# A projection computed by seven products of quarters, and a group norm applied by ScalarE, in a two-layer attention kernel

## The chip, the cores and the metric

The kernel runs on one core of a Trainium2 chip. A core has several engines with a queue of instructions each: TensorE (PE in the profile) multiplies matrices into PSUM banks of 128 partitions by 512 floats; VectorE (DVE) and ScalarE (ACT) work element by element on SBUF and PSUM; [...]SyncE (SP) mostly issues transfers (DMA). An engine takes its queue in order. An instruction that waits for another engine, or for a transfer, therefore holds up everything behind it in its own queue.

The metric is the time on the device in microseconds (us), the median over runs.

## The reference

The input is a batch of eight images, `x` of 8 x 512 x 32 x 32 in float32: 512 channels and T = 1024 positions per image. Two layers follow each other, cut here to what matters:

```python
# layer 0
h = group_norm(xf, gn_w, gn_b)                        # 32 groups of 16 channels
qkv = jnp.einsum('oc,bct->bot', qkv_w, h) + qkv_b[None, :, None]
q, k, v = jnp.split(qkv.reshape(b * 8, -1, T), 3, axis=1)   # 8 heads of 64 channels
q, k, v = fake_quant(q), fake_quant(k), fake_quant(v)       # to 255 levels, one scale per tensor
w = softmax(jnp.einsum('bct,bcs->bts', q * scale, k * scale), axis=-1)
a = jnp.einsum('bts,bcs->bct', w, v).reshape(b, c, T)
a = jnp.einsum('oc,bct->bot', proj_w, a) + proj_b[None, :, None]
x = xf + a
# layer 1, one head over all 512 channels
t = group_norm(x, gn_w, gn_b).reshape(B, C, T).transpose(0, 2, 1)
q, k, v = t @ wq.T + bq, t @ wk.T + bk, t @ wv.T + bv
attn = softmax(q @ k.transpose(0, 2, 1) / sqrt(C), axis=-1)
out = x + ((attn @ v) @ wp.T + bp).transpose(0, 2, 1)
```

## The kernel before

Until about 600 us a first phase computes q, k and v of all images and stores them to DRAM. The second phase, which the change touches, runs two streams of work side by side.

The first stream is the attention of layer 0, the generator `attention()`. Its units are (image b, pair of heads j, half hf of the queries, block s of 128 keys). A unit is a score matmul `st`, its exponential `pt` on ACT, a split of `pt` into a high and a low half of 16 bits (`two`, the low half by DVE; the high half by ACT or POOL), and the products `av` (with v) and `sm` (row sums). After all keys of a pair, `finish` copies the result to the `ao` tile, and `divide` (a DVE instruction, due about 20 us later) divides it by the row sums.

The second stream, `others()` (line 1900), takes image after image through the projection of layer 0 (`project`, line 1296), the group norm of layer 1 (`norm1`, line 1344) and the rest of layer 1 (`layer1`, line 1655). Layer 1 uses folded weights: `g` = (WqT Wk) h, scores `s` between g and h, values `v2ps` with Wp Wv, and `o`, the sum over the values. Each `yield` of this stream lets the attention go on by one step, so layer 1 of image b runs while the heads of image b+1 are attended to. The projection and norm of image b+1 run inside the last `o_run` of image b (`between`, line 1761): the projection's two halves after the fifth product of `o_run`'s seven, the two small steps of the norm after the sixth and seventh, the rest at the beginning of `layer1(b+1)`, whose first matmuls are `g` again.

**Seven products.** The blocks `g`, `v2ps`, `s` and `o` multiply two matrices by quarters. Each matrix is cut into 2 x 2 quarters, and seven products of sums of quarters give the result, where the plain form takes eight (Winograd's form of Strassen's method). The sums of the right-hand matrix (`t1 = h12 - h11`, `t2 = h22 - t1`, `h22 - h12`, `t4 = h21 - t2`) are formed by DVE; those of weights are formed once. The helper `seven` (line 1393) alternates between two PSUM banks, adds some products up in the bank, and lets a product wait (`awaits`) until the bank has been read. The work is tiled by 128 x 256: a product is 8 matmuls.

The projection of before is in plain form: for each half of the positions and each of four blocks of 128 output channels, four matmuls of 128 x 512 (`pj`) add up in a bank; DVE adds the bias and x, `evict`, into the `h` tile (`xts[b]`); a transfer stores it for layer 1's residual; and `bn_stats` takes the statistics for the norm. `norm1` gets the group means and variances through two tiny matmuls, and then DVE applies the norm in eight instructions of 128 x 512, four for each half, `(h - mean) * rstd`. The first half's four are issued at once, the second half's four are put off.

**Order.** A planner, the class `InOrder` (line 72), fixes the order of each engine's queue when the program is built. `dve`, `act` and `pe` each keep a planned time `t`. `do(cost, work)` issues an instruction now. `later(name, cost, work, ready, within)` puts a chore on a list with a time from which it may begin and one at which it is due. `fill` issues those chores that fit before a given time, the earliest first, and `settle(name)` issues all chores of that name at once, in their order:

```python
def do(self, cost, work, ready=None):
    ready = pe.t + 0.25 if ready is None else ready
    self.fill(ready)
    self.t = max(self.t, ready) + cost
    work()
```

The planner's costs are only estimates; the chip runs what was issued in the order in which it was issued. TensorE's order is that of the calls of `mm` (line 209 in the profile). Instructions issued through the planner are put down to line 91.

**Buffers.** The `h` tile holds x, then x plus the projection, then the normed input of layer 1. The tile `sums` holds the projection's weights (`wp`, 1 MB), and after the projection the sums of quarters of the normed input. Both are loaded late in layer 1 of the image before (line 1755). Scores and projection share the PSUM banks `ps_s`, of which `pair_ps` hands out two banks at a time; `g`, `v2ps`, `s` and `o` have the banks of `ps_o`.

Of the kernel before, what the change touches and what calls it, by code (L numbers as in the profile page):

```python
# [9 lines left out]
F32 = mybir.dt.float32  # L10
# [8 lines left out]
P = 128  # L19
# [39 lines left out]
def attn_pair_kernel(  # L59
# [166 lines left out]


    def norm_steps(
        src, dst, wcol, bank, nm, ccs=range(CC), fine=False, put=None, mv=None, apply=None
    ):  # L230

        n, c0 = len(ccs), ccs[0]
        put = put or (lambda hf, cost, work: work())
        if mv is None:
            st, mv = stat_tiles(n, nm)
            for i, cc in enumerate(ccs):
                for hf in range(NH):
                    dve.bn_stats(st[:, i, hf, :], src(cc, hf))  # L240
                aggregate(mv, st, i)
                if fine and i + 1 < n:
                    yield
        yield
# [12 lines left out]
        dve.do(0.6, offsets)  # L257
        yield
        ps2 = bank(f"gps2_{nm}")[:, 0:n]
        mm(ps2, lhsT=gavg, rhs=d, start=True, stop=True)  # L260
        rstd = small.tile([P, n], F32, tag=f"grstd{n}", name=f"grstd_{nm}")
        dve.do(0.15, lambda: dve.tensor_scalar(rstd, ps2, EPS, None, ALU.add))
        nc.gpsimd.tensor_tensor(rstd, rstd, mhalf[:, 0:n], ALU.pow)
        dve.do(
            0.15, lambda: dve.tensor_mul(rstd, rstd, vec[:, wcol + c0 : wcol + c0 + n]), dve.t + 1.4
        )
        if apply is not None:
            off = small.tile([P, n], F32, tag=f"goff{n}", name=f"goff_{nm}")
            dve.scalar_tensor_tensor(off, mean, -1.0, rstd, ALU.mult, ALU.mult)
            for i, cc in enumerate(ccs):  # L270
                apply(cc, rstd[:, i : i + 1], off[:, i : i + 1])
                yield
            return
        for hf in range(NH):
            for i, cc in enumerate(ccs):
                put(hf, 0.5, lambda i=i, cc=cc, hf=hf: dve.tensor_scalar(
                    dst(cc, hf), src(cc, hf), mean[:, i : i + 1], rstd[:, i : i + 1],
                    ALU.subtract, ALU.mult,
                ))
                if fine and i % 2 == 1:  # L280
                    yield
        if not fine:
            yield
# [23 lines left out]
    with ExitStack() as fast:  # L307
# [710 lines left out]
        def attention():  # L1018
# [138 lines left out]
            def finish(b, j, hf, u):  # L1157

                nm = f"{b}_{j}"
                if hf == 0:  # L1160
                    if b:
                        settle("ao")
                    ao[b, j] = aop.tile([P, NH, 512], F32, tag="ao", name=f"ao_{nm}")
                    if b == 0 and j % 2 == 1:
                        rss[b, j] = kept_u[:, 0:2].rearrange("p h k n -> p h (k n)")
                    else:
                        rss[b, j] = l1p.tile([P, NH, 512], F32, tag="rs", name=f"rs_{nm}")
                aot, rs = ao[b, j], rss[b, j]
# [15 lines left out]

                def divide():
                    dve.scalar_tensor_tensor(aot, aot, scl[:, 2:3], rs, ALU.mult, ALU.mult)

                def spread():
                    r = rcs[:, n * 16 : (n + 1) * 16]
                    dve.tensor_add(r, apart[:, 0, :], apart[:, 1, :])  # L1190
                    dve.reciprocal(r, r)
                    nc.sync.dma_start(rs_d[n].rearrange("r (p k) -> (r p) k", k=16), r)
                    for i, r in enumerate(HALF):
                        nc.sync.dma_start(
                            rs[r], rs_d[n][2 * i : 2 * i + 2, :].partition_broadcast(CH)
                        )
# [67 lines left out]
                dma(xts[b][:, :, bass.ts(hf, 512)], x_v[b, :, :, bass.ts(hf, 512)])  # L1264

        def load_wp(b, dma):
            wps[b] = l2p.tile([P, CC, C], F32, tag="sums", name=f"wp0_{b}")
            dma(wps[b], w_sq[WP0])

        def load_first(u):  # L1270

# [21 lines left out]
            for t, src in zip(wm_tiles(b), wm_d):  # L1293
                act.dma_start(t, src)

        def project(b, bank=bank):

            settle("ao")  # L1300
            st, mvs[b] = stat_tiles(CC, f"b{b}")
            wp0 = wps.pop(b)
            for hf in range(NH):
# [40 lines left out]
        def norm1(b, bank=bank):  # L1344
# [3 lines left out]

            def put(hf, cost, work):
                if hf == 0:  # L1350
                    dve.do(cost, work)
                else:
                    dve.later("h", cost, work, within=27.0)

            def put_sum(hf, i, work):
                if hf == 0:
                    dve.later("t4" if i == 3 else "t", elements(512), work, within=10.0 + 2.0 * i)
                else:
                    put(hf, elements(512), work)

            for n, _ in enumerate(norm_steps(
                at, at, V_GN1W, bank, f"b{b}", put=put, mv=mvs[b]
            )):
                if n == 2:
                    sums[b] = l2p.tile(
                        [P, 3, NH, CC // 2, 256], F32, tag="sums", name=f"sums2_{b}"
                    )
# [22 lines left out]
            dve.later("o", 0.25, spread, pe.t + 4.0, 5.0)  # L1390
            return rs

        def seven(nm, pairs, keep, whole, add, bank=bank):

            nonlocal turn
            turn ^= 1  # L1400
            x, y = (bank(f"{nm}_{i}").rearrange("p (t n) -> p t n", t=2) for i in range(2))

            def product(n, ps, start):
                left, right = pairs[n]
                k = left.shape[1]
                for t in range(2):
                    for i in range(k):
                        mm(
                            ps[:, t, :], lhsT=left[:, i, bass.ts(t, P)], rhs=right[:, i, :],
                            start=start and t == 0 and i == 0, stop=(i == k - 1),  # L1410
                            skip_group_check=True,
                        )
# [4 lines left out]
                (5, x, False, whole, None),  # L1417
            )
            for i, (n, ps, start, out, m) in enumerate(work):
                awaits(free[(i + turn) % 2])  # L1420
                product(n, ps, start)
                free[(i + turn) % 2] = out(ps) if m is None else out(m, ps)
                yield i + 1

        free = [0.0, 0.0]
        turn = 0

        def slots(gq):
# [226 lines left out]
        def layer1(b, steps):  # L1655
# [46 lines left out]
            for hf in range(NH):  # L1702
# [52 lines left out]
                if last and b + 1 < B:  # L1755
                    load_wp(b + 1, act.dma_start)
                    load_x2(b + 1, act.dma_start)
                if done >= B:
                    load_x1(b, hf, 0, 1, rx, aop)
                settle("v")  # L1760
                between = [lambda: iter((1,)), lambda: iter(()), lambda: iter(())]
                if b + 1 < B and last:

                    def first():
                        nonlocal ahead
                        yield -1
                        yield from project(b + 1, score_bank)
                        yield 2
                        ahead = norm1(b + 1, score_bank)
                        next(ahead)  # L1770
# [534 lines left out]
```

## Time and profile before

| | |
|---|---|
| time, median of 3 runs | 2559.91 us (2559.35 to 2560.78) |
| time of the profiled execution | 2559.32 us |
| its span, first to last instruction | 2557.2 us |
| granted TensorE clock, mean | 0.999 of full speed |
| HBM traffic over the span | 94 GB/s |
| PE busy, 0 to 600 us | 586.2 us |
| PE busy, 600 to 2400 us | 1782.7 us |
| PE busy, 2400 to 2557 us | 147.0 us |

Engines overlap, so busy times don't add up to the span. In the profile's timelines a line is a group of equal instructions close to each other: its start in us from the start of the span, the time from the start of its first to the end of its last instruction, the engine, the line of the code, the operation, output and inputs by the program's names, their shapes, and how many there are. Square brackets at the end hold the engine's idle time just before and what ended it. So `[5.64 <-PE st L209]` is an idle time of 5.64 us that ended when TensorE's `st` was there. In the table of groups the numbers after the bar are the whole busy time, the mean of one instruction in ns, and the idle time before them.

The projection's matmuls `pj` are 512 records with 224.1 us. The norms on DVE, 64 instructions, take 35.4 us in all: 0.455 us at the least, 0.538 in the median, 1.259 at the most.

### The profile page before, as it was taken

What the parts mean: (1) busy time and instruction counts of PE and PEld (TensorE: products, weight loads), DVE (VectorE), ACT (ScalarE), POOL (GpSimd) and SP (SyncE); (2) the same over time, 40 slices, a digit from 0 to 9 for tenths busy, and PEclk for the clock granted to TensorE, in tenths of its full rate; (3) what the DMA queues carried; (4) which work ended last, traced back from release to release, by engine and by line L of the source; (5) the groups of instructions that cost most, each with busy time, mean ns of one, the idle gap of its engine ahead of it and who ended that gap; (6) DMA issues with size and microseconds to landing.
All of it is one profiled execution on the core that took longest, in us unless ns stands there. A gap on an engine that the chain in (4) does not pass through costs nothing.

```text
span 2557.2 us, 38727 instructions
## 1 busy us (share of the span) xinstructions
PE 2515.9 (98%) x15670; PEld 1746.2 (68%) x15670; DVE 1897.6 (74%) x2747; ACT 1346.5 (53%) x1685; POOL 186.0 (7%) x167
## 2 busy tenths in 40 slices
PE   8999999999999999999999999999999999999998
PEld 4788888873357756775777577667756775777787
DVE  7887776668887778777877787777778777885544
ACT  3332223319857655665666466656655665664121
POOL 0000000001100001000100100010101000100000
PEclk9999999999999999999999999999999999999999
DMA  4533333236622232223313222322232123212211
GB/s 168 177 142 125 131 124 122 109 131 162 162 88 63 79 116 85 58 74 122 98 57 100 92 79 78 110 92 63 79 112 88 55 71 128 96 42 80 87 38 39
DMA packets 160717, 250.70 MB, mean 98 GB/s; under 512 B 27152, under 2 KB 93712, under 8 KB 159120
## 3 DMA queue, kind: packets, MB, share of 16 engines
q1 hardware_dynamic: 125792, 182.81, 21.6%
q10 hardware_dynamic: 30560, 57.71, 6.5%
q0 software_dynamic: 4176, 7.60, 1.7%
q8 instruction: 125, 2.05, 0.3%
q14 instruction: 64, 0.52, 0.1%
HBM read 153.64 MB, written 86.28 MB: 94 GB/s over the span
## 4 chain that ended last, share of the span: by engine, by line
PE 85%; DVE 5%; ACT 2%; issue 1%; DMA 1%; POOL 0%; SPq 0%; ACTq 0%; DVEq 0%
PE s L209 15%; PE o L209 13%; PE qkps L209 12%; PE pj L209 8%; PE av L209 8%; PE v2ps L209 7%; PE vps L209 6%; PE g L209 6%; PE st L209 4%; PE sm L209 3%; DVE two L91 2%; ACT pt L91 1%; PE fold L209 1%; DVE h L91 1%; DVE acc L91 0%
## 5 line engine op out<-in xcount | busy, mean ns | idle before, releaser
L91 ACT ACTIVATE pt<-st,esc 128x1024 f32<-128x1024 f32 x467 | 496.4, 1114 | 332.1 <-PE st L209 317.6
L91 DVE TENSOR_TENSOR two<-pt,two 128x1024 f16<-128x1024 f32 x467 | 561.5, 1216 | 131.0 <-POOL two L1092 100.7
L91 ACT CAST two<-pt 128x1024 f16<-128x1024 f32 x346 | 350.8, 1055 | 6.9 <-ACT p L91 5.1
L1092 POOL CAST two<-pt 128x1024 f16<-128x1024 f32 x112 | 146.0, 1304 | 1409.4 <-PE sm L209 746.3
L209 PE MATMUL av<-two,v 128*32 128x512 f16 x3968 | 245.9, 381 | 2.5 <-DVE two L91 2.1
L209 PE MATMUL s<-g,h 128*128 128x256 f32 x1024 | 233.4, 380 | 0.0
L209 PE MATMUL pj<-ao,wp 128*128 128x512 f32 x512 | 224.1, 595 | 0.6 <-DVE h L91 0.6
L209 PEld LDWEIGHTS s<-g,h 128*128 128x128 f32 x1024 | 192.9, 190 | 31.0 <-issue 4.3
L91 ACT ACTIVATE u_ring<-qkps,qkbt 128x512 f32<-128x512 f32 x89 | 60.9, 685 | 243.8 <-PE qkps L209 219.3
L209 PEld LDWEIGHTS <-v 128*32 128x32 f16 x3968 | 91.8, 96 | 140.0 <-issue 66.7
L209 PEld LDWEIGHTS pj<-ao,wp 128*128 128x128 f32 x512 | 96.0, 190 | 122.5 <-issue 110.8
L209 PE MATMUL s<-g,sums 128*128 128x256 f32 x768 | 178.4, 381 | 0.2 <-DVE p L91 0.2
L209 PE MATMUL o<-p,v 128*128 128x256 f32 x768 | 175.2, 382 | 1.0 <-DVE p L91 1.0
L209 PE MATMUL st<-q,k 64*128 64x512 bf16 x1024 | 163.4, 382 | 11.9 <-ACT pt L91 7.5
L209 PEld LDWEIGHTS o<-p,v 128*128 128x128 f32 x768 | 144.3, 190 | 27.1 <-issue 5.7
L209 PEld LDWEIGHTS s<-g,sums 128*128 128x128 f32 x768 | 144.7, 190 | 24.2 <-issue 4.6
L209 PE MATMUL sm<-two,ones 128*32 128x512 f16 x1984 | 136.0, 379 | 0.0
L209 PEld LDWEIGHTS <-k 64*128 64x128 bf16 x1024 | 34.8, 94 | 143.8 <-issue 142.2
L209 PE MATMUL qkps<-half,w_high 128*128 128x512 f32 x480 | 132.4, 398 | 0.0
L209 PE MATMUL qkps<-half,w_mix 128*128 128x512 f32 x480 | 130.6, 394 | 1.0 <-DVE half L91 1.0
L209 PE MATMUL qkps<-half,w_low 128*128 128x512 f32 x480 | 130.5, 394 | 0.0
L209 PE MATMUL v2ps<-wm,h 128*128 128x256 f32 x512 | 119.9, 383 | 1.9 <-ACT g L91 1.3
(226 smaller groups left out, 3902.2 us busy)
## 6 DMA issues: line engine op xcount, KB each, us to landing
rs<-rs_d SPq DMA_DIRECT2D x76, 256.0 KB
x<-in_x_dram SPq DMA_DIRECT2D x32, 512.0 KB
q_d<-wa SPq DMA_DIRECT2D x32, 512.0 KB
k_d<-wa SPq DMA_DIRECT2D x32, 512.0 KB
v_d<-v_ring SPq DMA_DIRECT2D x32, 512.0 KB
raw<-q_d SPq DMA_DIRECT2D x32, 512.0 KB
raw<-k_d SPq DMA_DIRECT2D x32, 512.0 KB
x_d<-h SPq DMA_DIRECT2D x64, 256.0 KB
```

The costliest lines, as they stand in the source:

```text
L91: ins = self.latest = op(*args, **kw).ins
L209: ins = nc.tensor.matmul(ps, lhsT=lhsT, rhs=rhs, **kw).ins
L1092: copy(two[:, 0], pt)
```

## The change

Two things are changed.

**The projection of images 1 to 7 in seven products.** `project` of image 0 stays as it was, but also has DVE form the four sums of the quarters of its weights (`combine_wp`), which are stored to DRAM. From the next image on, `load_wp` brings three quarters of the weights and three of the stored sums in three transfers of 1.5 MB in all; the fourth sum, 256 KB, comes into the room of layer 1's values by a transfer at the beginning of `project_seven`. The sums of quarters of `ao` are formed by DVE: the first two instructions after the division of the second pair of heads (`first_sums`), two more at the beginning of the projection, and four of 128 x 256 in each half. The bias is added to x beforehand, by four ACT instructions of 128 x 1024 (`add_bias`). The seven products of a half use the two banks of one `pair_ps` tile (`alone`), and each of them is added by DVE to its quarter of `h`, seven additions where there were four. The statistics of a half, four instructions, follow the sixth and seventh product; the stores are 256 wide.

**Layer 1's norm on ACT.** For all images the eight norms are ACT instructions with a scale and an offset, `h * rstd + off`; DVE computes the offset, one small instruction. Those of the first half are issued at once, and those of the second half are put on ACT's list (due within 22 us in place of 27). The four sums of quarters of each half stay on DVE. The second half's sums first settle all norms of that half.

```diff
     def norm_steps(
...
+        if scaled:
+            off = small.tile([P, n], F32, tag=f"goff{n}", name=f"goff_{nm}")
+            dve.do(0.15, lambda: dve.scalar_tensor_tensor(
+                off, mean, -1.0, rstd, ALU.mult, ALU.mult
+            ))
         for hf in range(NH):
             for i, cc in enumerate(ccs):
-                put(hf, 0.5, lambda i=i, cc=cc, hf=hf: dve.tensor_scalar(
-                    dst(cc, hf), src(cc, hf), mean[:, i : i + 1], rstd[:, i : i + 1],
-                    ALU.subtract, ALU.mult,
-                ))
+                if scaled:
+                    put(hf, 0.6, lambda i=i, cc=cc, hf=hf: act.activation(
+                        dst(cc, hf), src(cc, hf), AF.Identity, bias=off[:, i : i + 1],
+                        scale=rstd[:, i : i + 1],
+                    ))
...
                 def divide():
                     dve.scalar_tensor_tensor(aot, aot, scl[:, 2:3], rs, ALU.mult, ALU.mult)
+                    if b and j == 1:
+                        first_sums(b)
...
         def load_wp(b, dma):
-            wps[b] = l2p.tile([P, CC, C], F32, tag="sums", name=f"wp0_{b}")
-            dma(wps[b], w_sq[WP0])
+            wps[b] = w = l2p.tile([P, 6, CC // 2, C // 2], F32, tag="sums", name=f"wp0_{b}")
+            dma(w[:, 0:2].rearrange("p i k n -> p (i k) n"), w_sq[WP0][:, :, 0 : C // 2])
+            dma(w[:, 2], w_sq[WP0][:, CC // 2 :, C // 2 :])
+            dma(w[:, 3:6], wp_d[:, 0:3])
...
+        def combine_wp():
...
+            for args in (
+                (s1, a21, a22, ALU.add), (s2, s1, a11, ALU.subtract),
+                (s3, a11, a21, ALU.subtract), (s4, a12, s2, ALU.subtract),
+            ):
+                dve.later("wc", elements(512), lambda args=args: tt(*args), within=20.0)
+            dve.later("wc", 0.0, lambda: nc.sync.dma_start(wp_d, wc[:, 0:4]), within=20.0)
+
+        def add_bias(b):
+            for cc in range(CC):
+                act.later("xb", 1.05, lambda cc=cc: act.activation(
+                    xts[b][:, cc, :], xts[b][:, cc, :], AF.Identity,
+                    bias=vec[:, V_PB0 + cc : V_PB0 + cc + 1],
+                ), pe.t + 17.0, 24.0)
+
+        def first_sums(b):
+            for cc in range(CC // 2):
+                h = ao[b, cc]
+                dve.later("at", elements(512), lambda h=h: tt(
+                    h[:, :, 256:512], h[:, :, 256:512], h[:, :, 0:256], ALU.subtract
+                ), within=30.0)
+
+        def project_seven(b, room):
+
+            settle("at")
             settle("ao")
+            act.settle("xb")
...
+            act.dma_start(s4, wp_d[:, 3])
...
+            for k in range(2):
+                dve.do(elements(512), lambda k=k: second(k))
+
+            for hf in range(NH):
...
+                at = pair_ps(f"pj_{b}_{hf}")
+                banks = iter((at[:, 0, :], at[:, 1, :]))
+
+                def into(q, row, col, full, hf=hf):
+
+                    def add(ps):
+                        there = dve.do(elements(512), lambda: tt(q, ps, q, ALU.add))
+                        if full is not None:
+                            nc.sync.dma_start(x1_d[b][row][hf][:, :, col * 256 : (col + 1) * 256], q)
+                        return there
+
+                    return add
+
+                def stats(oc, hf=hf):
+                    dve.bn_stats(st[:, oc, hf, :], xts[b][:, oc, bass.ts(hf, 512)])
+                    if hf == NH - 1:
+                        aggregate(mvs[b], st, oc)
...
+                for step in seven(
+                    f"pj_{b}_{hf}",
+                    ((a11, h11), (a12, h21), (s2, th), (s3, h11), (s1, t1), (s4, h22), (a22, h21)),
+                    lambda n, ps: keeps[n](ps), into(q12, 0, 1, 1), lambda n, ps: adds[n](ps),
+                    lambda _: next(banks), True,
+                ):
+                    if step in (1, 2):
+                        for k in range(2):
+                            h = (h11, h21)[step - 1][k]
+                            args = (h, th[k], h) if step == 1 else (h, h, th[k])
+                            dve.do(elements(256), lambda args=args: tt(*args, ALU.subtract))
+                    for oc in {6: (2, 3), 7: (0, 1)}.get(step, ()):
+                        dve.later("pj", 0.62 + 0.2 * hf, lambda oc=oc, stats=stats: stats(oc), within=4.0)
+                    chore()
+                if hf + 1 < NH:
+                    yield -1
+            settle("pj")
...
             def put(hf, cost, work):
                 if hf == 0:
-                    dve.do(cost, work)
+                    act.do(cost, work, dve.t + 0.1)
                 else:
-                    dve.later("h", cost, work, within=27.0)
+                    act.later("h", cost, work, within=22.0)
 
             def put_sum(hf, i, work):
+
+                def sum_up():
+                    act.settle("h")
+                    work()
+
                 if hf == 0:
-                    dve.later("t4" if i == 3 else "t", elements(512), work, within=10.0 + 2.0 * i)
+                    dve.later(
+                        "t4" if i == 3 else "t", elements(512), work, act.t + 0.1, 10.0 + 2.0 * i
+                    )
                 else:
-                    put(hf, elements(512), work)
+                    dve.later("h", elements(512), sum_up, within=27.0)
...
-        def seven(nm, pairs, keep, whole, add, bank=bank):
+        def seven(nm, pairs, keep, whole, add, bank=bank, alone=False):
...
-            turn ^= 1
+            turn ^= not alone
+            free, side = ([0.0, 0.0], 0) if alone else (busy, turn)
...
                 if last and b + 1 < B:
                     load_wp(b + 1, act.dma_start)
                     load_x2(b + 1, act.dma_start)
+                    add_bias(b + 1)
...
-                        yield from project(b + 1, score_bank)
+                        yield from project(b + 1, vt)
```

More of the change, by code (lines that the diff above doesn't have):

```diff
@@ L228, in norm_steps @@
     def norm_steps(
-        src, dst, wcol, bank, nm, ccs=range(CC), fine=False, put=None, mv=None, apply=None
+        src, dst, wcol, bank, nm, ccs=range(CC), fine=False, put=None, mv=None, apply=None,
+        scaled=False,
     ):
@@ L273, in norm_steps @@
             return
+        if scaled:
[3 more added lines that the diff above has]
+            ))
         for hf in range(NH):
             for i, cc in enumerate(ccs):
-                put(hf, 0.5, lambda i=i, cc=cc, hf=hf: dve.tensor_scalar(
-                    dst(cc, hf), src(cc, hf), mean[:, i : i + 1], rstd[:, i : i + 1],
-                    ALU.subtract, ALU.mult,
-                ))
+                if scaled:
[3 more added lines that the diff above has]
+                    ))
+                else:
+                    put(hf, 0.5, lambda i=i, cc=cc, hf=hf: dve.tensor_scalar(
+                        dst(cc, hf), src(cc, hf), mean[:, i : i + 1], rstd[:, i : i + 1],
+                        ALU.subtract, ALU.mult,
+                    ))
                 if fine and i % 2 == 1:
@@ L1294, in load_wm @@
                 act.dma_start(t, src)
-        def project(b, bank=bank):
-            settle("ao")
+        wp_d = dram.tile([P, 4, CC // 2, C // 2], F32, tag="wp", name="wp_d")
+        def combine_wp():
+            wc = l2p.tile([P, 3, NT // 2, 256], F32, tag="vsum", name="wp_combined").rearrange(
+                "p a (s k) n -> p (a s) k n", k=2
+            )
+            a11, a12, a21, a22 = (
+                wps[0][:, k * CC // 2 : (k + 1) * CC // 2, m * 256 : (m + 1) * 256]
+                for m in range(2) for k in range(2)
+            )
+            s2, s3, s1, s4 = (wc[:, i] for i in range(4))
+            for args in (
[4 more added lines that the diff above has]
+            dve.later("wc", 0.0, lambda: nc.sync.dma_start(wp_d, wc[:, 0:4]), within=20.0)
@@ new lines, in project_seven, with second @@
+        def project_seven(b, room):
+            settle("at")
+            settle("ao")
+            act.settle("xb")
+            st, mvs[b] = stat_tiles(CC, f"b{b}")
+            w = wps.pop(b)
+            a11, a12, a22, s2, s3, s1 = (w[:, i] for i in range(6))
+            t2 = room[:, 0 : NT // 2, 0:256].rearrange("p (k h) n -> p k h n", h=NH)
+            s4 = room[:, NT // 2 : NT // 2 + 2, 0:256]
+            act.dma_start(s4, wp_d[:, 3])
+            left, right = slice(0, 256), slice(256, 512)
+            def second(k):
+                tt(t2[:, k], ao[b, 2 + k][:, :, right], ao[b, k][:, :, right], ALU.subtract)
+            for k in range(2):
+                dve.do(elements(512), lambda k=k: second(k))
+            for hf in range(NH):
+                h11, t1, h21, h22 = (
+                    [ao[b, c + k][:, hf, n] for k in range(2)] for c in (0, 2) for n in (left, right)
+                )
+                th = [t2[:, k, hf] for k in range(2)]
+                q11, q12, q21, q22 = quarters(b, hf)
+                at = pair_ps(f"pj_{b}_{hf}")
[11 more added lines that the diff above has]
+                        aggregate(mvs[b], st, oc)
+                keeps = [into(q, *at_, None) for q, at_ in ((q11, (0, 0)), (q21, (1, 0)), (q22, (1, 1)))]
+                adds = [into(q, *at_, 1) for q, at_ in ((q11, (0, 0)), (q21, (1, 0)), (q22, (1, 1)))]
+                for step in seven(
[15 more added lines that the diff above has]
+            settle("pj")
+            for k in [k for k in ao if k[0] == b]:
+                del ao[k]
@@ L1301, in project @@
+        def project(b, room=None):
+            if b:
+                yield from project_seven(b, room)
+                return
+            settle("ao")
+            combine_wp()
             st, mvs[b] = stat_tiles(CC, f"b{b}")
@@ L1350, in put @@
                 if hf == 0:
-                    dve.do(cost, work)
+                    act.do(cost, work, dve.t + 0.1)
                 else:
-                    dve.later("h", cost, work, within=27.0)
+                    act.later("h", cost, work, within=22.0)
             def put_sum(hf, i, work):
+                def sum_up():
+                    act.settle("h")
+                    work()
                 if hf == 0:
-                    dve.later("t4" if i == 3 else "t", elements(512), work, within=10.0 + 2.0 * i)
+                    dve.later(
+                        "t4" if i == 3 else "t", elements(512), work, act.t + 0.1, 10.0 + 2.0 * i
+                    )
                 else:
-                    put(hf, elements(512), work)
+                    dve.later("h", elements(512), sum_up, within=27.0)
             for n, _ in enumerate(norm_steps(
-                at, at, V_GN1W, bank, f"b{b}", put=put, mv=mvs[b]
+                at, at, V_GN1W, bank, f"b{b}", put=put, mv=mvs[b], scaled=True
             )):
                 if n == 2:
+                    if b == 0:
+                        settle("wc")
                     sums[b] = l2p.tile(
@@ L1408, in product @@
                         mm(
-                            ps[:, t, :], lhsT=left[:, i, bass.ts(t, P)], rhs=right[:, i, :],
+                            ps[:, t, :], lhsT=left[:, i, bass.ts(t, P)],
+                            rhs=right[i] if type(right) is list else right[:, i, :],
                             start=start and t == 0 and i == 0, stop=(i == k - 1),
@@ L1419, in seven @@
             for i, (n, ps, start, out, m) in enumerate(work):
-                awaits(free[(i + turn) % 2])
+                if not alone:
+                    side = turn
+                awaits(free[(i + side) % 2])
                 product(n, ps, start)
-                free[(i + turn) % 2] = out(ps) if m is None else out(m, ps)
+                free[(i + side) % 2] = out(ps) if m is None else out(m, ps)
                 yield i + 1
-        free = [0.0, 0.0]
+        busy = [0.0, 0.0]
         turn = 0
```

## The prediction

> **What bounds the kernel now.** I read the page's table of busy times first, then TensorE's timeline through one image, then the timelines of VectorE (DVE) and ScalarE (ACT) beside it.
>
> ```profile
> span 2557.2 us, 38727 instructions
> ...
> PE 2515.9 (98%) x15670; PEld 1746.2 (68%) x15670; DVE 1897.6 (74%) x2747; ACT 1346.5 (53%) x1685; POOL 186.0 (7%) x167
> ```
>
> TensorE (PE) is busy 98% of the span, so any microsecond that PE waits is added to the end, and any that it no longer works is taken off. One image between 1171 and 1410 us shows it: PE busy 237.8 of 239.0 us. What must be priced is PE work saved against new waits of PE. TensorE's timeline around the second half of the projection of image 2, counted from 0 (the other steady images repeat it 240 us apart):
>
> ```profile
> 1189.54 14.00 PE L209 MATMUL pj<-ao,wp 128*128 128x512 f32 x32
> 1203.47 1.05 PE L209 MATMUL av<-two,v 128*32 128x512 f16 x16
> 1204.45 0.61 PE L209 MATMUL st<-q,k 64*128 64x512 bf16 x4
> 1204.98 0.61 PE L209 MATMUL sm<-two,ones 128*32 128x512 f16 x8
> 1205.42 1.03 PE L209 MATMUL av<-two,v 128*32 128x512 f16 x16
> 1206.29 0.60 PE L209 MATMUL sm<-two,ones 128*32 128x512 f16 x8
> 1206.83 0.62 PE L209 MATMUL st<-q,k 64*128 64x512 bf16 x4
> 1207.38 3.72 PE L209 MATMUL o<-g,vsum 128*128 128x256 f32 x16
> ...
> 1221.62 0.60 PE L209 MATMUL st<-q,k 64*128 64x512 bf16 x4
> 1222.16 3.72 PE L209 MATMUL g<-h,wa 128*128 128x256 f32 x16
> ```
>
> No row shows an idle time: DVE and ACT are just in time everywhere. They have gaps, but their queues are in order, so where new work stands in a queue matters more than how much of it there is. I therefore took the order of the changed program's instructions on each engine and laid the durations of this trace on it.
>
> **A. The seven products: a gain.** A half of the projection takes 1203.47 - 1189.54 = 13.93 us. A product of two quarters is 8 records of 128x256; the timeline of the score block has 16 of them starting at 1131.79 and the next at 1135.24, 1.73 us a product, and 1.75 with the change of bank. Seven take 12.2 us: 1.73 us less per half, 3.5 us per image, 24 us over images 1 to 7. Image 0 keeps its old form.
>
> **B. Within the halves: no wait.** DVE must take each product out of its bank within the next product's 1.75 us. An add of 128x512 follows its neighbour by 0.61 to 0.65 us, the two subtractions of 256 behind products 1 and 2 take about 0.36 us each (half-way down from 0.61 at 512, with the stream's fixed part). 0.15 + 0.65 + 0.72 us fit. The score matmul after the first half waits 0.52 us for the last eviction now (row at 1185.86) and still does. The bias of x moves to ACT before the projection (two of its four instructions, 1.15 us each): ACT is idle 3.48 us before 1166.63, and the x load, which with 0.5 MB more weights ends about 1.3 us later than 1158.8 (at the 390 GB/s of 1150 to 1158), is there. If it came 3 us later still, that cover would be gone and exps and scores would slip by what is missing. I take 0, at most 1 us.
>
> **C. The tail of the second half: a wait.** In VectorE's timeline now:
>
> ```profile
> 1188.90 1.23 DVE L91 TENSOR_TENSOR two<-pt,two 128x1024 f16<-128x1024 f32 x1 [0.93 <-POOL two L1092]
> ...
> 1194.06 0.69 DVE L91 BATCH_NORM_STATS2 gst_b<-h 128x6 f32<-128x512 f32 x1
> 1194.79 0.21 DVE L91 BATCH_NORM_AGGREGATE gmv_b<-gst_b 128x2 f32<-128x12 f32 x1
> 1194.91 1.17 DVE L91 TENSOR_TENSOR two<-pt,two 128x1024 f16<-128x1024 f32 x1
> ```
>
> The `two` (the low half of the exps) that PE's `av` at 1205.42 needs was ready at 1190.1. In the changed order this one and the next stand behind the second half's last eviction and three statistics with their aggregates. From the end E of the last product: 0.15 to see it, 0.65 eviction, 3 x 0.85 (1194.06 to 1194.91), 1.2 for `two`, 0.1 to hand over: E + 4.65. PE gets there at E + 2.17 (1205.42 - 1203.47, and 0.22 for the part that needs only the high half): 2.5 us. The next `two` comes 1.14 later, with 0.44 of PE work between: 0.7. **3.2 us** per image; 2.4 if the statistics overlap better, 3.6 at most.
>
> **D. The norm on ACT: a wait.** No row of the steady stage shows this operation there; the nearest is layer 0's norm of image 0, the same form (scale and offset from SBUF, 128x512):
>
> ```profile
> 26.78 1.52 ACT L91 ACTIVATE x<-x,goff,rstd 128x512 f32<-128x512 f32 x2 [2.18 <-DVE goff L91]
> ...
> 1218.82 2.12 ACT L91 ACTIVATE pt<-st,esc 128x1024 f32<-128x1024 f32 x2 [5.64 <-PE st L209]
> ```
>
> Two in 1.52 us with the second's own 0.80: 0.72 us apart. In the changed order **all eight** stand ahead of the two exps of 1218.82, although only four are wanted at once: the DVE chore that forms the second half's first sum is begun early and settles them. Count from O = 1207.38, the start of `o`. The scale was ready, and the norm began, at 1218.01 (O + 10.63); with the new offset and the hand-over at O + 10.9. Eight: O + 16.6. Exps of 1.06: done at O + 17.7 and O + 18.75. The score matmuls at 1221.62 (O + 14.24) write the banks that these two exps read: the first waits 3.5 us, the second 0.8 more. **4.3 us**.
>
> A rule of the Trainium skill speaks against this part: "ScalarE: Activation LUTs", Rules for kernel authors, has adds and multiplies done on VectorE rather than ScalarE. Another speaks for it: "Perfetto Trace Analysis", Optimizing Scalar/DVE Operations, lets ScalarE take work where DVE is saturated. DVE is busy 28.45 of 29.04 us from 1222.16 on, but only 10.05 of 14.78 us just before, where ACT now stands in the way, so the first decides. The cycle table of "VectorE: DVE Perf Modes", errata section, has 224 + 512 cycles at 1.2 GHz, 0.61 us: eight would end at O + 15.8 and the wait be 3.5 us, not 4.3. I take the row. At the 0.54 of an exp from SBUF with a constant scale it would be 3.0.
>
> **E. DVE's queue behind it: a wait.** That first sum of the second half also stands at the head of DVE's queue and waits for the sixth norm, O + 15.3; DVE idles 4.4 us where it had no gap. Behind it, before the add that frees the second bank of `g`: six sums (3.8), `o`'s eviction (0.6), three `two` (3.4), the division (1.2), two residual adds (0.8), one more difference (0.6) and the add itself (0.6): O + 26.3. PE wants that bank for the fourth product of `g`: scores until O + 19.1, three products of 1.75: O + 24.4. **1.9 us**; 0 if the rows behind run 15% quicker, 2.5 at most.
>
> **Image 0** has only D's part: four norms and the copy of the last fold (0.5) now stand ahead of the exps of 730.80, and the score at 730.95 needs that copy: 3.8 us, and about 1 for the later four. Forming and storing the combined weights (four adds, 2.6 us of DVE) has DVE's idle 2.39 us before 715.77. **Image 7** has no attention beside it: gain 27.47 - 24.3 = 3.2; its `o` bank is freed behind the sixth norm and the sums come after it, some 4.4 us of waits, and 1.0 in the projection's end: +2.2.
>
> **Sum.** Images 1 to 6: -3.5 + 3.2 + 4.3 + 1.9 = +5.9 each, 35.4. With 4.8 and 2.2: +42 us on the profiled execution's own 2559.32 us (span 2557.2), which is 0.6 under the median of 2559.91: **2602 us**, 1.7% slower.
>
> **Rivals.**
> - *The saving stands* (faster): DVE reaches the late `two` and ACT the exps in time. For it speaks that DVE is 74% and ACT 53% busy, and that the work moved is small; against it the order on the queues. It decides where C, D and E together fall under 3.5 us per image; with none of them 2559.3 - 24 = 2535. Chance 0.17.
> - *One wait in place of the gain*: the projection's tail costs its 3.2 us and the norm block little, because PE comes to its scores late anyway: about 2558. Against it: D is counted from PE's own position, so a late PE doesn't shrink it. 0.06.
> - *The norm alone*: `two` is in time and D and E stay: +2.7 each, 16 + 7 = 2582; or D and C without E: 2591 and somewhat below, if the norm runs at 0.6. 0.22.
> - *A backlog*: DVE, saturated from 1222 on, carries E's delay into the next blocks, or the x load holds ACT: 8 or 9 us per image, 2618. 0.08.
> - The forecast as summed, 2590 to 2612: 0.47.
>
> What can be told from no change is 0.2%, 5 us. Faster 0.17, same 0.06, slower 0.77. The range, 2556 to 2616, takes in the one wait in place of the gain, the partial cases, C, D and E at both ends, and leaves out the first rival and the top of the backlog; the likeliest alone is 2590 to 2612.
>
> **What would show it.** PE's busy time of `pj` falls from 224 to about 207 us (28 for image 0, and 7 x 112 records of 0.228 us, the 233.4 / 1024 of the score block's row). In each steady image PE shows three new idle times: in `av` after the second half, ended by DVE's `two`; at `st` before `g`, ended by ACT's `pt`, near 3.5 and 0.8 us; in `g`, ended by DVE. The eight norms on ACT lie in one run of about 5.7 us ahead of two exps. I am wrong if the idle at `st` ended by `pt` sums to under 10 us over the kernel, if the norm takes under 0.6 us, or if a half of seven products takes over 13 us.

## The result, and the profile after

The changed kernel takes **2734.05 us** (median of 4 runs, 2733.72 to 2737.81), the kernel before 2560.35 us in its 4 runs: 1.0682 times as long, with a 95% interval of 1.0664 to 1.0701. The forecast was 2602 us, 2556 to 2616: the direction was right, the size was not. It was 42 us slower by forecast, and 174 us by measurement.

The page of the kernel after, its span and busy times (PEld is TensorE's loading of weights; POOL is GpSimd, whose casts of 128x1024 for the high halves took 1.30 us on average in the kernel before, ScalarE's 1.06):

```profile
span 2735.9 us, 39670 instructions
...
PE 2558.6 (94%) x16006; PEld 1822.1 (67%) x16006; DVE 1937.4 (71%) x2821; ACT 1423.1 (52%) x1777; POOL 181.2 (7%) x167
```

TensorE did not get less to do by the records (2558.6 us busy, 2515.9 before), and it is no longer busy all the time: 177 us of the span are left, where there were 41. What it waited for in the second phase is in the view of waits (waiting instruction, releaser, total us, times, longest); these are the largest rows:

```profile
PE pj L209 <- DVE h L91: 73.0, 85, 4.0
PE st L209 <- ACT pt L91: 31.1, 33, 3.1
PE av L209 <- DVE two L91: 22.6, 21, 2.0
PE g L209 <- DVE g L91: 4.4, 4, 1.2
```

The second, third and fourth row are the waits that the prediction named in D, C and E. In the kernel before the same view has 6.7, 2.1 and none. The first row was not in the prediction at all: the matmuls of the projection wait 85 times for DVE's evictions, before 0.6 us in all.

The timeline of TensorE through image 2 shows where each lies:

```profile
1209.27 1.99 PE L209 MATMUL pj<-ao,wp 128*128 128x256 f32 x8
1212.04 1.99 PE L209 MATMUL pj<-ao,wp 128*128 128x256 f32 x8 [0.78 <-DVE h L91]
1214.82 1.99 PE L209 MATMUL pj<-v,wp 128*128 128x256 f32 x8 [0.78 <-DVE h L91]
...
1256.20 0.61 PE L209 MATMUL av<-two,v 128*32 128x512 f16 x8 [2.04 <-DVE two L91]
1257.33 0.40 PE L209 MATMUL av<-two,v 128*32 128x512 f16 x4 [0.52 <-DVE two L91]
...
1259.08 4.90 PE L209 MATMUL o<-g,vsum 128*128 128x256 f32 x16
...
1277.67 0.39 PE L209 MATMUL st<-q,k 64*128 64x512 bf16 x2 [3.10 <-ACT pt L91]
1278.67 0.61 PE L209 MATMUL st<-q,k 64*128 64x512 bf16 x2 [0.61 <-ACT pt L91]
1279.21 5.07 PE L209 MATMUL g<-h,wa 128*128 128x256 f32 x16
...
1287.16 1.99 PE L209 MATMUL g<-h,wa 128*128 128x256 f32 x8 [1.14 <-DVE g L91]
```

Cut at the starts of the same instructions in both kernels, image 2 gives this table (us):

| stretch | before | after | change | forecast |
|---|---|---|---|---|
| first half of the projection | 13.93 | 18.66 | +4.73 | -1.73 |
| scores and values behind it | 4.59 | 4.92 | +0.33 | 0 |
| second half of the projection | 13.93 | 18.97 | +5.04 | -1.73 |
| from there to `o` (C) | 3.91 | 7.26 | +3.35 | +3.2 |
| three pairs of products of `o` | 11.00 | 12.19 | +1.19 | 0 |
| from there to `g` (D) | 3.78 | 7.94 | +4.16 | +4.3 |
| `g`, its first seven products (E) | 10.56 | 13.33 | +2.77 | +1.9 |
| sum | | | +21.57 | +5.9 |

The whole period of an image, from one first norm matmul to the next, is 263.55 us where it was 240.22, so 1.8 us more lie outside these rows. C, D and E came near their sizes; how far that is luck stands further below. The projection's two halves alone are 13.2 us per image off the forecast, and 7 x 13.2 = 92 us of the 132 that it missed.

### The profile page after: what moved, and what is told of

It is laid out like the page before. It is cut to its first block, busy times and chain, and to the rows that moved or that the text cites. A ratio compares the mean times of both kernels' runs of the same rounds, so it can differ in the third digit from the quotient of the medians.

```text
span 2735.9 us, 39670 instructions
## 1 busy us (share of the span) xinstructions
PE 2558.6 (94%) x16006; PEld 1822.1 (67%) x16006; DVE 1937.4 (71%) x2821; ACT 1423.1 (52%) x1777; POOL 181.2 (7%) x167
## 4 chain that ended last, share of the span: by engine, by line
PE 77%; DVE 11%; ACT 4%; DMA 2%; issue 2%; POOL 0%; ACTq 0%; SPq 0%; DVEq 0%
PE s L209 14%; PE o L209 13%; PE qkps L209 11%; PE pj L209 7%; PE v2ps L209 7%; PE av L209 6%; PE vps L209 6%; PE g L209 5%; PE st L209 4%; DVE two L91 3%; PE sm L209 3%; DVE h L91 3%; ACT pt L91 1%; ACT h L91 1%; DVE gst_b L91 1%
## 5 line engine op out<-in xcount | busy, mean ns | idle before, releaser
L91 DVE TENSOR_TENSOR two<-pt,two 128x1024 f16<-128x1024 f32 x467 | 569.2, 1241 | 143.9 <-POOL two L1104 81.4
L209 PE MATMUL av<-two,v 128*32 128x512 f16 x3968 | 253.4, 384 | 27.0 <-DVE two L91 22.6
L209 PE MATMUL pj<-ao,wp 128*128 128x256 f32 (+1 forms) x624 | 169.7, 416 | 51.1 <-DVE h L91 51.1
L209 PE MATMUL st<-q,k 64*128 64x512 bf16 x1024 | 169.6, 390 | 39.5 <-ACT pt L91 31.9
L209 PEld LDWEIGHTS pj<-ao,wp 128*128 128x128 f32 x624 | 113.7, 191 | 106.3 <-DVE h L91 74.7
L91 DVE TENSOR_TENSOR h<-pj,h 128x512 f32<-128x512 f32 x98 | 67.6, 690 | 128.6 <-PE pj L209 126.0
L209 PE MATMUL g<-h,wa 128*128 128x256 f32 x512 | 134.6, 415 | 7.1 <-DVE g L91 4.4
```

The lines of the kernel that those rows point to most:

```text
L91: ins = self.latest = op(*args, **kw).ins
L209: ins = nc.tensor.matmul(ps, lhsT=lhsT, rhs=rhs, **kw).ins
```

## The experiments

**What holds the products up.** The timeline with VectorE beside TensorE, from the end of the first product (1209.27, above) to the start of the second:

```profile
1211.30 0.69 DVE L91 TENSOR_TENSOR h<-pj,h 128x512 f32<-128x512 f32 x1 [0.67 <-PE pj L209]
1211.91 0.75 DVE L91 TENSOR_TENSOR ao<-v,ao 128x256 f32<-128x256 f32 x2
1212.04 1.59 PEld L209 LDWEIGHTS pj<-ao,wp 128*128 128x128 f32 x8 [1.18 <-DVE h L91]
1212.04 1.99 PE L209 MATMUL pj<-ao,wp 128*128 128x256 f32 x8 [0.78 <-DVE h L91]
```

The second product goes into the other bank, and yet it begins only when DVE has taken the first one out (1211.30 + 0.69 = 1211.99). PE and DVE take turns: 1.99 us of product, 0.78 us of waiting, 2.78 us a product in place of 1.75. The new code takes both banks as halves of one tile (`pair_ps`), where the other blocks in seven products take two tiles. The first experiment changes that alone (`score_bank` asks for a `pair_ps` tile and uses its first bank, so two calls give two tiles):

```diff
-                at = pair_ps(f"pj_{b}_{hf}")
-                banks = iter((at[:, 0, :], at[:, 1, :]))
...
-                    lambda _: next(banks), True,
+                    score_bank, True,
```

> The changed kernel with one edit: the two banks of a half of the projection come from two tiles (score_bank twice) in place of the two halves of one pair_ps tile. Theory 'one tile': each product waits for the eviction of the one before it only because both banks belong to one tile. Then the idle 0.78 us before each of the 12 later products goes and the pace falls from 2.78 to about 1.75 us a product; the two halves, 18.7 and 19.0 us in image 2, become about 12.3 each, 13 us less per image, 91 over images 1 to 7: about 2643 us. Rival 'DVE hand-over': a product waits for sums or evictions that it really needs, and PE and DVE can't overlap here whatever the tiles: the pace stays at 2.78 and the time at about 2734. Rival 'displaced': the pace falls, but DVE, now later, makes PE wait in av and g instead, and less than half of the 91 us comes back: over 2690.

Measured: 2640.16 us, 93.9 less than the changed kernel. Its timeline of TensorE, the second half of image 2's projection:

```profile
1211.69 3.72 PE L209 MATMUL pj<-ao,wp 128*128 128x256 f32 x16
1215.25 1.89 PE L209 MATMUL pj<-v,wp 128*128 128x256 f32 x8
1216.98 5.34 PE L209 MATMUL pj<-ao,wp 128*128 128x256 f32 x24
1222.16 1.89 PE L209 MATMUL pj<-ao,v 128*128 128x256 f32 x8
```

Seven products without a wait, 12.3 us from the first to what follows, as A and B of the prediction had them. Over the second phase `pj` waits 3.9 us for DVE where it waited 73.0. Both rivals fall: PE and DVE do overlap with two tiles, and the time isn't lost again elsewhere. The built programs' lists of waits say the same of the second half's second product (here of image 3), which writes a bank that no product of this half has yet used:

```
changed    Matmult pj_3_1   <- ao_3_2, wp0_3  128x256  [waits DVE]
two tiles  Matmult pj_3_1_1 <- ao_3_2, wp0_3  128x256  [waits Activation]
```

With two tiles it waits for ScalarE, whose exponential was the last to read that bank; with one tile it waits for VectorE, which is just reading the other one.

**What the norm on ScalarE costs.** Two runs, once taken from the changed kernel and once added to the kernel before:

```diff
# norm on VectorE (the changed kernel without this part)
-                    act.do(cost, work, dve.t + 0.1)
+                    dve.do(cost, work)
...
-                    act.later("h", cost, work, within=22.0)
+                    dve.later("h", cost, work, within=27.0)
...
-                at, at, V_GN1W, bank, f"b{b}", put=put, mv=mvs[b], scaled=True
+                at, at, V_GN1W, bank, f"b{b}", put=put, mv=mvs[b]
```

> The changed kernel with layer 1's norm applied by DVE again, as before; the seven products stay as they are. Theory 'the norm's waits add': the stretches from the scores before g to the end of g's first seven products are 4.16 and 2.77 us longer per image with the norm on ACT, and both go: 7 x 6.9 and about 4 of image 0, 52 us, so about 2682. Rival 'displaced': with the projection late, the time is lost elsewhere anyway: over 2715. Rival 'part of it': only the three waits themselves go (3.10 + 0.61 + 1.14), not PE's slow microseconds after them: about 2696.

> The kernel before with only the norm's part of the change: eight norms of 128x512 on ACT with scale and offset, the projection in plain form. Theory 'the norm's waits add': D and E of the prediction with what PE loses after them, 6.9 us per image, and about 4 in image 0: 2560 + 52 = about 2612; as the prediction summed D and E, without the slow microseconds, 6.2 x 6 + 4.8 + 4.4 = about 2606. Rival 'only behind a late projection': the norm's waits come from ACT and DVE being late behind the new projection, and alone they cost little: under 2580.

Measured: 2673.68 us, which is 60.4 under the changed kernel, and 2620.74 us, which is 60.0 over the kernel before in the same session (2560.75). The two agree, so the norm's cost does not hang on the new projection; it is 8 us more than the 52 expected. The timeline of TensorE with the norm alone on ScalarE, image 2:

```profile
1244.08 0.39 PE L209 MATMUL st<-q,k 64*128 64x512 bf16 x2 [3.32 <-ACT pt L91]
1245.08 0.61 PE L209 MATMUL st<-q,k 64*128 64x512 bf16 x2 [0.61 <-ACT pt L91]
1245.62 4.89 PE L209 MATMUL g<-h,wa 128*128 128x256 f32 x16
...
1253.56 1.99 PE L209 MATMUL g<-h,wa 128*128 128x256 f32 x8 [1.32 <-DVE g L91]
```

The same three waits as in the changed kernel, at the same places. That the number of norms ahead of the exps makes them was tested with four norms on ScalarE instead of eight:

```diff
-                if scaled:
+                if scaled and hf == 0:
                     put(hf, 0.6, lambda i=i, cc=cc, hf=hf: act.activation(
...
-                    act.later("h", cost, work, within=22.0)
+                    dve.later("h", cost, work, within=27.0)
...
-                def sum_up():
-                    act.settle("h")
-                    work()
```

> The kernel before with only the first half's four norms on ACT; the second half's four and their sums stay on DVE as before. Theory D and E ('the four that aren't wanted yet stand ahead of the exps'): the two exps come 4 x 0.72 = 2.9 us earlier than with all eight on ACT, so the waits of 3.1 and 0.6 us before g fall to under 1 us together, and DVE has no instruction waiting for the sixth norm: about 1 us per image, and some 6 in image 0, where the four norms and the last fold's copy stand ahead of the exps: 2567, at most 2575. Rival 'the norm on ACT itself': what costs is the way over ACT (offset, hand-over, 0.72 in place of 0.54 us each), not the number ahead of the exps: over 2590.

Measured: 2577.2 us, 17 over the kernel before (2560.23). Its timeline of TensorE, the waits of image 0 and image 2:

```profile
735.94 0.61 PE L209 MATMUL st<-q,k 64*128 64x512 bf16 x2 [3.90 <-ACT wm L91]
```

```profile
1231.11 0.39 PE L209 MATMUL st<-q,k 64*128 64x512 bf16 x2 [0.50 <-ACT pt L91]
1232.11 0.39 PE L209 MATMUL st<-q,k 64*128 64x512 bf16 x2 [0.61 <-ACT pt L91]
```

The wait of 3.32 us is 0.50, 2.8 us less against 2.9 by D's working, and the wait in `g` is gone. So the second half's four norms, which nobody wants yet, and DVE's sum behind the sixth norm cost 43.5 us of the 60 (2620.74 - 2577.2). The way of the first four over ScalarE costs 1.3 to 2.1 us per image, from one first norm matmul to the next, and 5.7 us in image 0. The time is 2 us over the upper end that was expected. One rival stays open: the run takes the four norms off ScalarE altogether, so it doesn't separate their place ahead of the exps from the time that they take there. No run left all eight on ScalarE with the last four behind the exps.

**Whether the parts add.** Both edits together:

> The changed kernel with both edits: two tiles for the banks, and the norm on DVE. Theory 'they add': 2734 - 91 - 52 = about 2591. What is left over the kernel before is then the wait behind the statistics, the ACT queue ahead of the projection, and the gain of the products: 4.5 + 1.5 - 3.2 us per image, 2560 + 20 = 2580 at the best. Rival 'the saving stands': with both gone it is the pure gain of the seven products, 2535 to 2545.

Measured: 2581.33 us, within 1.6 us of what adding the two measured gains gives (2734.05 - 93.9 - 60.4 = 2579.8), and far from the pure saving. What is left are two waits. One stands ahead of the projection and was forecast at nothing; the timeline of the changed kernel there:

```profile
1184.41 1.80 ACTq L91 DMA_DIRECT2D wp<-in_w_sq_dram  x2
...
1186.25 0.48 ACTq L91 DMA_DIRECT2D wp<-wp_d  x1
1186.77 1.00 ACTq L91 DMA_DIRECT2D h<-in_x_dram  x2
1187.85 0.58 ACT L91 COPY kept_u<-o 128x512 f32<-128x512 f32 x1 [2.86 <-PE o L209]
1188.34 1.12 ACT L91 ACTIVATE pt<-st,esc 128x1024 f32<-128x1024 f32 x1
1189.34 1.04 ACT L91 CAST two<-pt 128x1024 f16<-128x1024 f32 x1
...
1190.44 0.40 PE L209 MATMUL av<-two,v 128*32 128x512 f16 x4 [0.68 <-ACT two L91]
...
1191.70 0.40 PE L209 MATMUL av<-two,v 128*32 128x512 f16 x4 [0.86 <-DVE two L91]
```

The lines of ACTq are transfers that ScalarE issues. It issues five, 1184.41 to 1187.77, where it issued three in 1.39 us; the timeline of ScalarE in the kernel before:

```profile
1148.06 0.35 ACTq L91 DMA_DIRECT2D wp<-in_w_sq_dram  x1
1148.45 1.00 ACTq L91 DMA_DIRECT2D h<-in_x_dram  x2
1149.50 1.05 ACT L91 CAST two<-pt 128x1024 f16<-128x1024 f32 x1 [0.85 <-ACT p L91]
```

There the cast follows the transfers at once. In the changed kernel it also stands behind a copy and an exponential; TensorE wants its result and waits. The next run fetches the weights by one transfer; image 0 stores the three plain quarters beside the combined ones for it:

```diff
-            dma(w[:, 0:2].rearrange("p i k n -> p (i k) n"), w_sq[WP0][:, :, 0 : C // 2])
-            dma(w[:, 2], w_sq[WP0][:, CC // 2 :, C // 2 :])
-            dma(w[:, 3:6], wp_d[:, 0:3])
+            dma(w, wp_d[:, 0:6])
...
+            for m, quarter in enumerate((a11, a12, a22)):
+                nc.sync.dma_start(wp_d[:, m], quarter)
```

> Two tiles, the norm on DVE, and one more edit: image 0 stores the three plain quarters of the weights beside the combined ones, so that a later image fetches its six quarters by one transfer in place of three, and ACT issues three DMAs there as before, not five. Theory 'ACT's issues': the two additional issues, 3.35 us on ACT's queue in place of 1.39, put the cast of one block late, for which PE waits 0.68 and then 0.86 us in av, shortly ahead of the projection of every image: 1.5 us x 7, about 11 us less than 2581, 2570. Rival 'the bias': ACT is late there because of the bias of x, which stays: 2578 or more.

Measured: 2568.07 us (8 runs, 2564.63 to 2571.74), 13.3 less. The two waits are gone from its timeline, where all 32 products with v follow each other, and the bias, which stayed, is not their cause:

```profile
1151.50 1.91 PE L209 MATMUL av<-two,v 128*32 128x512 f16 x32
```

The other wait is C, behind the statistics. The last run of this line moves `settle("pj")` behind the attention step that follows the projection:

```diff
-            settle("pj")
             for k in [k for k in ao if k[0] == b]:
                 del ao[k]
...
                         yield 2
+                        settle("pj")
                         ahead = norm1(b + 1, score_bank)
```

> The kernel of the one load, with the second half's statistics put off until after the attention step behind the projection: four low halves (two) of the exps come before the last three statistics on DVE. Theory 'behind the statistics': the wait of 2.04 us in av behind the second half, and what PE loses after it, go; the stretch from there to o falls from 7.8 to about 3.9 us, 3.9 x 7 = 27 us less: about 2543. If all else is covered it is the saving of the seven products alone, 7 x 3.3 = 23 us under the kernel before: 2537. Rival 'the wait moves': the statistics are now late for the norm's first matmul, which stands behind the next product of o, and PE waits there: over 2555.

Measured: **2551.68 us** (2550.79 to 2552.21), 16.4 less than with one load, and 0.9964 times the kernel before, with an interval of 0.9950 to 0.9978. This version is faster than both kernels, by a small margin over the one before. Its gain is 8.5 us, not the 23 of the seven products, and the time lies between the two that were expected. Its timeline of TensorE, image 2:

```profile
1202.64 0.40 PE L209 MATMUL av<-two,v 128*32 128x512 f16 x4 [0.34 <-DVE two L91]
...
1208.29 0.36 PE L209 MATMUL gps_b<-gmv_b,gavg 128*128 128x4 f32 x2 [0.40 <-DVE gmv_b L91]
...
1225.26 1.99 PE L209 MATMUL g<-h,wa 128*128 128x256 f32 x8 [0.22 <-DVE g L91]
```

The wait of 2.04 us is 0.34; in its place stand several of a few tenths. The rival of the moved wait is right in kind (PE does wait at the norm's first matmul), not in size. The last run tried to take that wait away:

```diff
                     two(split, u + 6)
+                    dve.settle("pj")
                     two(scores, u + 8)
                 elif dense:
```

> The kernel of the late statistics, with the last three statistics two low halves earlier on DVE: behind the two that the second half's av wants, ahead of the two that later exps want. In the kernel of the late statistics PE waits 0.40 us for the statistics at the norm's first matmul and loses some 0.1 after it, in six images. Theory: this wait goes, 0.5 x 6 = 3 us less than 2551.7, about 2548.5. Rival 'the exps': the later exps now stand behind the statistics, and PE waits for them before the products of o or in av: 2551 or more.

Measured: 2559.36 us (13 runs, 2555.22 to 2562.45), no different from the kernel before (2559.98 in that session) and slower by 7.7 than the version it was to better. The theory misses; the rival has the time (2551 or more) but not the place: the wait for the statistics is gone and the exps are in time, but the timeline of TensorE has new waits later, in `g`:

```profile
1224.61 1.99 PE L209 MATMUL g<-sums,wa 128*128 128x256 f32 x8 [0.35 <-ACT vsum L91]
1227.40 1.99 PE L209 MATMUL g<-h,wa 128*128 128x256 f32 x8 [0.79 <-DVE g L91]
```

Which of the moved instructions makes these late was not followed further.

## Why the prediction was wrong

**B is the step that failed**: "Within the halves: no wait." It priced whether DVE is quick enough for each bank (0.15 + 0.65 + 0.72 us in 1.75), which it is, and took for granted that a product waits only for its own bank. It waits for the tile, and the tile is both banks. What was in plain sight: the diff takes `at[:, 0, :]` and `at[:, 1, :]` of one tile where every other block asks twice for a bank, and in the changed program's list of waits the second product of a half waits for DVE, though nothing of its bank or its operands is DVE's to finish. The Trainium skill, "PSUM — Partial Sum Buffer", in its section on bank collisions, has PSUM guarded by semaphores for each bank and quadrant; so the chip does not ask for this wait, and the run with two tiles, whose products run while DVE reads the other bank, agrees: 2640.16 us. With B mis-taken, A's gain of 3.5 us per image became a loss of 9.8. The point named beforehand as a sign of error, a half of seven products over 13 us, is met with 18.7; and `pj`'s busy time is 227 us, not 207, since a product that can't overlap its neighbour takes 1.99 us.

**B's second line** (the bias and the larger load: 0, at most 1 us) was mis-sized too: the load's two additional issues cost 13.3 us in the kernel. The prediction weighed when the data lands, and not the instructions that issue the transfers, which take ScalarE's own time.

**C** (3.2 us) was right in place and mechanism: the two waits are 2.04 and 0.52 us, 2.56 together. The timeline of VectorE in the changed kernel has the statistics ahead of `two` as foreseen:

```profile
1254.18 0.64 DVE L91 BATCH_NORM_STATS2 gst_b<-h 128x6 f32<-128x512 f32 x1
1254.85 0.21 DVE L91 BATCH_NORM_AGGREGATE gmv_b<-gst_b 128x2 f32<-128x12 f32 x1
1254.97 5.41 DVE L91 TENSOR_TENSOR two<-pt,two 128x1024 f16<-128x1024 f32 x4
```

**D and E** (4.3 and 1.9 us) were right in mechanism; the waits themselves, 3.10 and 0.61, then 1.14 us, are shorter than forecast. The timelines of ScalarE and VectorE in the changed kernel:

```profile
1270.88 0.81 ACT L91 ACTIVATE h<-h,goff_b,grstd_b 128x512 f32<-128x512 f32 x1 [5.49 <-DVE goff_b L91]
...
1271.60 5.02 ACT L91 ACTIVATE h<-h,goff_b,grstd_b 128x512 f32<-128x512 f32 x7
1276.53 4.09 ACT L91 ACTIVATE pt<-st,esc 128x1024 f32<-128x1024 f32 x4
```

```profile
1275.24 0.69 DVE L91 TENSOR_TENSOR sums<-h 128x512 f32<-128x512 f32 x1 [4.40 <-ACT h L91]
```

Eight norms 0.72 us apart, in 5.7 us, ahead of the exps; DVE idle for 4.4 us, the very figure of the prediction. The choice between the row of layer 0 (0.72) and the estimate of 0.61 from the cycle table of the Trainium skill's "VectorE: DVE Perf Modes", errata section, was right for the row. Yet the norm cost 60 us (61.7 between the profiled spans) where the terms sum to 46 (6.2 x 6, 4.8 and 4.4).

**A term that was missing** explains that difference: after a long wait TensorE can run slowly. The windows of the changed kernel (stretch, its length, busy us of PE, PEld, DVE, ACT and POOL with the count, the granted clock, DMA share, GB/s):

```profile
1256.00:1258.00 2.00, 1.28 (x20) 0.45 (x19) 2.00 (x3) 1.74 (x2) 0.58 (x1) 1.00 0.03 8
1258.00:1262.00 4.00, 4.00 (x16) 2.65 (x13) 3.52 (x3) 3.12 (x5) 1.31 (x1) 0.57 0.00 0
1262.00:1264.00 2.00, 2.00 (x13) 1.77 (x11) 0.00 (x0) 2.00 (x4) 0.00 (x0) 1.00 0.01 1
```

The clock is 0.57 for 4 us, from 0.7 us behind the second wait in `av`; the 16 matmuls of `o` take 4.90 us for 3.72. It is the same behind the wait before `g`, where 16 take 5.07. The run with the norm alone on ScalarE shows what this adds up to, since it has the same 15670 matmuls as the kernel before:

```profile
PE 2537.9 (97%) x15670; PEld 1756.8 (67%) x15670; DVE 1869.4 (71%) x2691; ACT 1391.8 (53%) x1749; POOL 176.8 (7%) x167
```

Of its span of 2618.9 us TensorE is idle for 81.0, where it was idle for 41.3: 39.7 us more, less than the 46 of the terms. The other 22.0 us are the same matmuls being busy for longer (2537.9 for 2515.9). An estimate from the clock in the windows of 8 us that begin at the ends of its seven waits of 3.3 to 3.9 us (0.57 to 0.79) puts 15 of them there. That C, D and E came near their sizes in the table is thus in part luck: the waits were shorter than forecast, and the slow clock, which the prediction left out, filled the difference.

Not every such wait brings it. The wait of 2.04 us in `av` stands in images 1 to 6 of five of the runs with seven products. Over the 7 us from its end the mean clock is 0.53 to 0.77 in 22 of these 30 places and 1.00 in the other 8, as in image 2 with two tiles, where the same 16 matmuls of `o` take 3.72 us:

```profile
1228.37:1235.37 7.00, 6.43 (x45) 4.52 (x45) 5.90 (x5) 6.06 (x7) 1.90 (x1) 1.00 0.01 2
```

Behind the waits of 3.1 us or more at `st` (images 0 to 6 of the changed kernel, of the norm alone and of two tiles) it is 0.57 to 0.79 over 8 us in all 21 places. What else decides stays open; no run changed the clock alone. The Trainium skill, "TensorE: Matmul & The Clock Gate", Part 1, has the clock halved after a window of about 3.4 us without work. Here 2.04 and 0.52 us of waiting could suffice, and the measurement decides.

The parts as the runs have them, from 2734.05 downward: one tile 93.9, the norm on ScalarE 58.8 (between the two runs with two tiles), the issues 13.3, the statistics 16.4. They leave 2551.7. The rival "the saving stands" (2535) fell. Where the last 15 us of the seven products' gain stay is known only in part: in the fastest version TensorE is idle for 50.2 us where it was 41.3 before, so some 9 of them are such waits as its timeline shows, of 0.2 to 0.4 us.

## What to carry to other kernels

Two buffers are two only if whatever orders the instructions knows them as two: before pricing a double buffer, look in the list of waits for what its second use waits for. Count what a change issues on every queue, transfers as well as arithmetic, and price waits of TensorE of 2 us and more above their length, since the slow clock can come after. On queues in order, look where work that nobody wants yet will stand: the four norms of the second half on ScalarE, ahead of exps that were wanted, cost 43.5 us, more than the whole saving.

## What was not expected of the hardware

The clock can fall after short waits: in the changed kernel a wait of 2.04 us, or of 3.10 us, is followed by about 4 us at 0.57 of the clock, while six waits of 0.78 to 0.85 us in a row, with 1.99 us of work between them, leave it at 1.00 (1209.20 to 1228.00 us). The same wait of 2.04 us leaves it at 1.00 in 8 of 30 places. And five issues of transfers hold ScalarE's queue for 3.4 us, 0.5 to 0.9 us each.
